# Turning column order into row order in three parts of 64 channels instead of two

## The chip, the cores and the metric

The kernel is one program on one core of a Trainium2 chip. Its time is the device time of one execution, in microseconds. The core has five engines that run their own instruction streams in order: TensorE (PE in the profile), VectorE (DVE), ScalarE (ACT), GpSimd (POOL) and SyncE (SP), which issues all DMAs of this kernel.

## What is computed

Four layers over 4 images of 96 channels and 64 x 64 pixels. Only layer 0 matters here. It is a state-space scan: a depthwise convolution gives `u` with 192 channels, which is read in four orders (rows, columns, and both backwards). In each order a recurrence with 16 states per channel runs over the 4096 positions, and the four results, put back into row order, are added with `Ds` times the input:

```python
def step(hst, inp):
    ut, dt_, bt, ct = inp
    dA = jnp.exp(dt_[..., None] * A[None])
    hst = hst * dA + (dt_ * ut)[..., None] * bt[:, :, None, :]
    y = jnp.einsum('bkdn,bkn->bkd', hst, ct)
    return (hst, y)
...
ys = ys + Ds.reshape(K, DI)[None, :, :, None] * xs
y0 = ys[:, 0].reshape(b, DI, h, w)
y1 = ys[:, 1].reshape(b, DI, w, h).transpose(0, 1, 3, 2)
y2 = jnp.flip(ys[:, 2], -1).reshape(b, DI, h, w)
y3 = jnp.flip(ys[:, 3], -1).reshape(b, DI, w, h).transpose(0, 1, 3, 2)
y = y0 + y1 + y2 + y3
```

A layer norm over the channels and a matrix product follow. Layer 1 is an inverted-bottleneck convolution, layer 2 a Fourier-domain mixer and a feed-forward block, layer 3 linear attention and a feed-forward block.

## The kernel before

**The scan** is the backbone (`scans`, L1216 on). For each image, each order k (0 rows, 1 columns, 2 and 3 backwards) and each of 8 chunks of 512 positions there is a step of 12 slots; 1536 slots in all. A slot handles 64 channels by 8 states in two tiles of 128 x 512. GpSimd forms `db` (L1274), ScalarE the decays `da` (L1284) and copies of the last state (L1308), VectorE runs the recurrence (L1293) and in seven slots of twelve the product with C (L1298). In the other five GpSimd forms that product (L1314). PE sums over the states into the bank `ps_y` (L1338). SP loads the replicated inputs `rep_BC`, `rep_d` and `rep_g` (L1243, L1249) half a step to a step ahead. The result of a step goes to the DRAM tensor `d_y[k]`, 256 rows: rows 0 to 127 are channels 0 to 127, while channels 128 to 191 are there twice, as partial sums over half of the states each, in rows 128 to 191 and 192 to 255.

**Everything else is side work.** Each stage ("front", "turn", "conv", "spectral", "layer_2", "layer_3", "layer_3_turn") is a few Python generators that yield an engine and a planned cost ahead of the instructions they emit. After the scan's own instructions of a slot, `advance` (L1459) takes steps of the first unfinished stage as long as the slot's allowance lasts (L57, `SHARE`: 3.0 us of PE a slot, at most 3.2 saved up; 2.4 of ScalarE; 1.5 of VectorE). A step is taken if half of its cost is left (`fits`, L1446). `yield wait(n)` lets n slots pass. A stage starts only when the one before it is finished. `WORK` (L54) holds the planned cost of each stage, for the rate at which side work is taken. The order of instructions on every engine is that in which they are emitted. Stores are put on a list (`later`) and issued at the next slot's start on the same SP queue as the loads. `in_turn` (L456) emits the matmuls of an item and, one item later, its evacuation; `ahead(1, ...)` (L448) issues an item's loads one item early.

The plan is: front of images 0, 1, 2, then for image 0 turn, conv, spectral, layer 2 and layer 3; front of image 3; the same for image 1, with the turn of image 2 as one stream beside its layer 3; the same for image 2, with the turn of image 3; and last conv and the rest of image 3. What is not done when the scan ends is done after it with all engines free.

**The turn** (`turn`, L631) takes the results of the two column orders, k = 1 and 3, and adds them in row order, together with the forward row order (k = 0) and `Ds` times the input (`d_skip`). It needs three orders of its image to be scanned; for image 3, whose column orders are scanned first, only two, and the rows that wait for order 0 come second. It runs in two parts: channels 0 to 127, and rows 128 to 255. A part has two big tiles, `ya` and `yb` of 128 x 6144 f32. The first 4096 columns of each receive one column order (L641, two DMAs of 2 MB). After `wait(10)` the eight chunks follow: loads of 512 columns of `d_y[0]` (L649) and of `d_skip` (L650) into the spare columns of the tiles, two matmuls whose moving operand steps through the tile column by column (L662; 256 bytes between elements), one with the row order (L664) and one with the skip (L665), whose stationary operand is a diagonal of `Ds`. The stationary operand of the others is an identity, or in the second part two identities of 64 stacked (`two`), which add rows 128 to 191 and 192 to 255. ScalarE copies the sum out (L669), and it is stored to `d_yt`. `scan_outputs` (L679) reads that with the backward row order and begins the "conv" stage.

Of the kernel before, what the change touches and what calls it, by code (L numbers as in the profile page):

```python
# [19 lines left out]
F32 = mybir.dt.float32  # L20
# [3 lines left out]
ALU = mybir.AluOpType  # L24
AX = mybir.AxisListType
PSUM = bass.MemoryType.PSUM

B, C, H, W = 4, 96, 64, 64
L = H * W
# [21 lines left out]

WORK = {"weights": 47.0, "turn": 70.0, "front": 417.0, "conv": 447.0,  # L54
        "spectral": 111.2, "layer_2": 231.0, "product": 1.2, "layer_3": 153.6, "layer_3_turn": 223.6}
RATE = 6.0
SHARE = {"pe": (3.0, 3.2), "act": (2.4, 2.8), "dve": (1.5, 2.0)}  # L57
NQ, NG, NPAIR = 4, HID // 32, H // 2


COLS = [
    ("convb_a", 1), ("convb_b", 1), ("ds_a", 4), ("ds_b", 4), ("one", 1),
    ("lng_a", 1), ("lng_b", 1), ("lnb_a", 1), ("lnb_b", 1),
# [32 lines left out]
def hybrid_kernel(ctx: ExitStack, tc: tile.TileContext, a: dict):  # L96
# [45 lines left out]
    def const(name, rows=slice(0, 128)):  # L142
        return cst[rows, CS[name]]
# [40 lines left out]
    def big(name):  # L184
        if last_room and turns(thirds) == "last":
            return last_room[0].tile([128, 6144], F32, name=name, tag="big", bufs=1)
        return bp.tile([128, 6144], F32, name=name, tag="big", bufs=2)
# [6 lines left out]
    def tmp(name, shape=(128, CH), dtype=F32):  # L194

        if last_room and dtype == F32:
            tag = turns(spare)
            if tag in LAST:
                return last_room[0].tile([128, CH], F32, name=name, tag=tag, bufs=LAST[tag])[:, : shape[1]]
        return bp.tile(list(shape), dtype, name=name, tag="tmp", bufs=TMP)  # L200
# [33 lines left out]
    def split(t):  # L234
        return t.rearrange("p (a b) -> p a b", a=RPC)
# [11 lines left out]
    dtw = small.tile([128, K, DI], F32, name="dtw")  # L247
    taps = small.tile([128, 9, DI], F32, name="taps")
    aneg = small.tile([128, 96], F32, name="aneg")
    ds_a = small.tile([128, 1], F32, name="ds_a")  # L250
    ds_b = small.tile([128, 1], F32, name="ds_b")
    skips = small.tile([128, 2, 128], F32, name="skips")
    w1 = small.tile([128, HID], F32, name="w1")
    w2 = small.tile([128, NT1 + 1, C], F32, name="w2")
    wkv = small.tile([128, 2 * C], F32, name="wkv")
# [29 lines left out]
    def first_weights():  # L285

        take = scratch(big("weights"))

        win = take(128, DI)
        load(win, a["win_t"])  # L290
        load_row(taps.rearrange("p t d -> p (t d)"), "convw")
        load(sel, a["sel"])
        load(dtw, a["dtw"])
        load(cst[:, : CS["grp"].start], a["cst"][:, : CS["grp"].start])
        load(cst[:, CS["grp"].stop :], a["cst"][:, CS["grp"].stop :])
        nc.vector.tensor_copy(ident16, const("ident", slice(0, C))[:, :C])
        nc.vector.tensor_mul(taps, taps, win.unsqueeze(1).to_broadcast([128, 9, DI]))

        pre = take(128, NPRE)
        load(pre, a["pre"])  # L300
        act(aneg, pre[:, PRE["alog"]], AF.Exp)
        nc.vector.tensor_scalar(aneg, aneg, -1.0, None, ALU.mult)
        nc.vector.reduce_sum(ds_a, cols[:, COL["ds_a"]], axis=AX.X)


        nc.vector.memset(ds_b, 1.0)
        nc.vector.reduce_sum(ds_b[:64], cols[:64, COL["ds_b"]], axis=AX.X)
        nc.vector.tensor_scalar(skips[:, 0], const("ident"), ds_a, None, ALU.mult)
        nc.vector.tensor_scalar(skips[:, 1], const("two"), ds_b, None, ALU.mult)

    def later_weights():

# [124 lines left out]
    def later(out, t, then=None):  # L437

        to_store.append((out, t, then))
# [16 lines left out]
    def in_turn(items, make, matmuls, take, evict, depth=2, ready=None):  # L456


        made = []

        def oldest():
            p, item, at = made.pop(0)
            yield take[:3] + (at,)
            evict(p, item)
            free()

        items, n = iter(items), 0
        while True:
            while ready is not None and not ready(n):
                yield wait(1)  # L470
            item = next(items, None)
            if item is None:
                break
            yield make[:3] + (n > 0,)
            p = bank()
            matmuls(p, item)
            made.append((p, item, clock[0]))
            n += 1
            if len(made) == depth:
                yield from oldest()  # L480
        while made:
            yield from oldest()
# [148 lines left out]
    def turn(b):  # L631


        im = b % 2
        early = b == B - 1
        while scanned[b] < (2 if early else 3) * NCH:
            yield wait(1)
        parts = [big("ya"), big("yb")]
        for lo in (128, 0) if early else (0, 128):
            for t, k in zip(parts, (1, 3)):  # L640
                load(t[:, :L].rearrange("p (c l) -> p c l", c=NCH),  # L641
                     d_y[k][im][:, lo : lo + 128, :].rearrange("c p l -> p c l"))

            rows = not (early and lo == 128)

            def fetch(c):
                y, u = (t[:, L + c % 4 * CH : L + c % 4 * CH + CH] for t in parts)
                if rows:
                    load(y, d_y[0][im][c, lo : lo + 128])  # L649
                load(u[: min(128, DI - lo)], d_skip[b][c, lo : min(lo + 128, DI)])  # L650
                return y, u

            whole = lo == 0
            m, add = (128, const("ident")) if whole else (64, const("two")[:, :64])
            skip = skips[:, 0] if whole else skips[:64, 1, :64]

            def added(p, of):
                c, (y, u) = of
                p = p[:m]
                for n, t in enumerate(parts):  # L660
                    rhs = t[:, :L].rearrange("p (w h) -> p h w", h=H)[:, c * RPC : (c + 1) * RPC, :]
                    mm(split(p), lhsT=add, rhs=rhs, start=n == 0, stop=False)  # L662
                if rows:
                    mm(p, lhsT=add, rhs=y, start=False, stop=False)  # L664
                mm(p, lhsT=skip, rhs=u[: skip.shape[0]], start=False, stop=True)  # L665

            def stored(p, of):
                s = tmp("yrow")[:m]
                nc.scalar.copy(s, p[:m])  # L669
                later(d_yt[im][of[0]][lo : lo + m], s)  # L670

            chunks = ahead(1, fetch, range(NCH))

            ready = (lambda n: scanned[b] >= 2 * NCH + min(n + 2, NCH)) if early and rows else (lambda n: True)
            yield wait(10)
            yield from in_turn(chunks, pe(3.8, 1), added, ac(0.6), stored, ready=ready)
            yield wait(2)

    def scan_outputs(b, done):  # L679
# [865 lines left out]
def _layout(v):  # L1545
# [12 lines left out]
    def rows128(x, first=0):  # L1558

        return np.pad(x, [(first, 128 - first - x.shape[0])] + [(0, 0)] * (x.ndim - 1))  # L1560
# [13 lines left out]
    for o in (0, 1):  # L1574
# [1 line left out]
    w2 = tiles(l1["w2"].T, NT1)  # L1576
    cols = {
        "convb_a": l0["conv_b"][:128], "convb_b": np.tile(l0["conv_b"][128:], 2), "one": one,
        "ds_a": ds[:128], "ds_b": ds[128:],
        "lng_a": l0["ln_g"][:128], "lng_b": l0["ln_g"][128:],  # L1580
        "lnb_a": l0["ln_b"][:128], "lnb_b": l0["ln_b"][128:],
        "alog": l0["A_logs"].reshape(K, NI // 2, 32, 2, NJ, 4).transpose(2, 5, 0, 1, 3, 4).reshape(128, 96),
# [68 lines left out]
```

## Time and profile before

| | |
|---|---|
| Median of 3 runs | 6392.89 us (6386.3 to 6405.43) |
| The profiled execution | 6409.81 us |
| Its span, first to last instruction | 6408.0 us |
| Busy: VectorE, GpSimd, PE, ScalarE | 5488.4, 5171.1, 4763.2, 4178.6 us |
| Moved by DMA | 1112 MB, 174 GB/s on average |

The profile gives the instructions of one execution with start, length, line and tile, and for idle time the instruction or DMA that ended it. An f32 matmul is there as two records. Slots can be counted by the L1274 products: the four turns' first column loads are at 1384, 3069, 4201 and 5416 us, in slots 298, 748, 1062 and 1387, and the last product of the scan starts at 5963 us. The trace has no landing times for DMAs, but it has each packet's length.

### The profile page before, as it was taken

To read this page: it belongs to the slowest core of one execution; us is meant where nothing else is said; L and a number is where in the kernel's file an instruction comes from. 1 tells how busy PE (TensorE), PEld (TensorE's weight loads), DVE (VectorE), ACT (ScalarE), POOL (GpSimd) and SP (SyncE) were. 2 spreads that over 40 slices of the span, in tenths; PEclk is the share of its full clock that TensorE was granted. 3 is DMA by queue.
4 is the path that set the end of the run, shared out by engine and by line. 5 is a ranking of instruction groups with operands and counts; after the bars stand their busy time and mean duration, and the time that the engine had idled before them with its cause. 6 is when DMAs were issued, how large, how long until landed. Compare 5 with 4: busy or idle time off the path is not lost. (4 is left out here: it accounts for less than half of the span.)

```text
span 6408.0 us, 84715 instructions
## 1 busy us (share of the span) xinstructions
PE 4763.2 (74%) x27804; PEld 1766.1 (28%) x27804; DVE 5488.4 (86%) x6059; ACT 4178.6 (65%) x8040; POOL 5171.1 (81%) x2743
## 2 busy tenths in 40 slices
PE   6633767757987776686589877767988786867998
PEld 2100212111223532121122254211223632112274
DVE  5979898988999889999899988988999889799345
ACT  5743777765675677887566667856675677665435
POOL 4757878878999889987999988987999888899200
PEclk9855978868998877797799988878998877878999
DMA  5644565666644544456775455465644545555201
GB/s 186 210 159 148 184 205 194 200 222 230 190 158 157 193 161 144 162 195 213 250 222 170 150 180 174 144 213 186 195 161 153 198 157 174 185 188 181 95 11 42
DMA packets 434365, 1112.01 MB, mean 174 GB/s; under 512 B 72474, under 2 KB 74240, under 8 KB 432772
## 3 DMA queue, kind: packets, MB, share of 16 engines
q1 hardware_dynamic: 433924, 1106.58, 52.5%
q8 instruction: 221, 3.62, 0.2%
q14 instruction: 220, 1.80, 0.1%
HBM read 873.41 MB, written 237.44 MB: 173 GB/s over the span
## 5 line engine op out<-in xcount | busy, mean ns | idle before, releaser
L1274 POOL TENSOR_TENSOR db<-rep_g,rep_BC 128x1024 f32<-128x1024 f32 x1536 | 3608.6, 2365 | 753.4 <-DVE hc L1293 352.1
L1284 ACT ACTIVATE ps_da<-rep_d,aneg 128x512 f32<-128x512 f32 x3072 | 2062.6, 690 | 460.1 <-DVE hc L1293 351.1
L1293 DVE TENSOR_TENSOR_SCAN ps_da<-ps_da,state,db 128x512 f32<-128x512 f32 x1568 | 1922.4, 1271 | 284.8 <-ACT state L1308 166.3
L1314 POOL TENSOR_TENSOR hc<-hc,rep_BC 128x1024 f32<-128x1024 f32 x640 | 1511.0, 2361 | 48.5 <-DVE hc L1293 3.7
L1293 DVE TENSOR_TENSOR_SCAN hc<-ps_da,state,db 128x512 f32<-128x512 f32 x1120 | 1370.8, 1264 | 135.2 <-issue 41.7
L1338 PE MATMUL ps_y<-hc,cst 128*32 128x512 f32 x6144 | 1004.1, 732 | 524.2 <-POOL hc L1314 215.6
L1298 DVE TENSOR_TENSOR hc<-ps_da,rep_BC 128x512 f32<-128x512 f32 x1792 | 1133.7, 673 | 0.2
L1308 ACT COPY state<-ps_da 128x1 f32<-128x1 f32 x1568 | 247.3, 158 | 452.9 <-DVE hc L1298 452.1
L1338 PEld LDWEIGHTS ps_y<-hc,cst 128*32 128x32 f32 x6144 | 147.3, 118 | 1173.2 <-issue 484.6
L818 PE MATMUL ps_mm<-h,wd 128*32 128x512 f32 x3144 | 359.9, 593 | 7.0 <-ACT r L155 7.0
L552 PE MATMUL ps_mm<-xp,taps 128*128 128x512 f32 x576 | 292.2, 651 | 47.6 <-ACT xp L532 14.2
L1293 DVE TENSOR_TENSOR_SCAN ps_da<-ps_da,db 128x512 f32<-128x512 f32 x224 | 261.0, 1210 | 28.4 <-ACT state L1308 14.3
L795 PE MATMUL ps_mm<-wd,w 128*32 128x512 f32 x2016 | 255.4, 622 | 27.6 <-DMA wd<-x 17.0
L603 PE MATMUL ps_mm<-xd,dtw 128*128 128x512 f32 x256 | 167.4, 745 | 71.1 <-ACT z L625 51.8
L1293 DVE TENSOR_TENSOR_SCAN hc<-ps_da,db 128x512 f32<-128x512 f32 x160 | 186.1, 1203 | 22.9 <-issue 16.4
L877 PE MATMUL ps_mm<-r,cst 128*128 128x512 f32 x214 | 148.9, 785 | 55.8 <-ACT acc L900 20.3
L799 ACT ACTIVATE h<-ps_mm 128x512 f32<-128x512 f32 x267 | 155.7, 596 | 51.9 <-PE ps_mm L795 49.3
L705 PE MATMUL ps_mm<-ypart,cst 128*128 128x512 f32 (+1 forms) x272 | 158.0, 704 | 38.1 <-DMA ypart<-yt 37.4
L990 PE MATMUL ps_mm<-wa,xp 128*64 128x96 f32 x1728 | 135.1, 318 | 66.2 <-DVE d L995 56.6
L618 DVE SCALAR_TENSOR_TENSOR ps_mm<-ps_mm,z 128x512 f32<-128x512 f32 x192 | 131.3, 684 | 60.5 <-ACT z L616 57.7
L612 ACT ACTIVATE z<-ps_mm 128x512 f32<-128x512 f32 x192 | 114.2, 595 | 96.6 <-PE ps_mm L603 48.2
L552 PEld LDWEIGHTS ps_mm<-xp,taps 128*128 128x128 f32 x576 | 115.4, 207 | 222.0 <-issue 158.8
(343 smaller groups left out, 6824.3 us busy)
## 6 DMA issues: line engine op xcount, KB each, us to landing
rep_BC<-bc SPq DMA_DIRECT2D x512, 512.0 KB
rep_g<-du SPq DMA_DIRECT2D x384, 512.0 KB
rep_d<-delta SPq DMA_DIRECT2D x384, 512.0 KB
y<-yt SPq DMA_DIRECT2D x512, 128.0 KB
du<-g SPq DMA_DIRECT2D x128, 256.0 KB
delta<-z SPq DMA_DIRECT2D x128, 256.0 KB
tab<-in_etab SPq DMA_DIRECT2D x112, 256.0 KB
ypart<-y SPq DMA_DIRECT2D x72, 256.0 KB
```

What stands on the lines that cost most here:

```text
L552: mm(p, lhsT=taps[:, t, 0:128], rhs=window(t, c + e), start=t == 0, stop=t == 8)
L603: mm(p, lhsT=dtw[:, o + 2 * part, 0:128], rhs=xd, start=True, stop=True)
L705: mm(p, lhsT=const(name, slice(0, s.shape[0])), rhs=s, start=n == 0, stop=n == len(of) - 1)
L795: mm(p[32 * n : 32 * n + 32], lhsT=w1[:, 32 * g : 32 * g + 32], rhs=xin[:, n : n + 15 : 2, 1 : W + 1], start=True, stop=True)
L818: mm(p[32 * n : 32 * n + 32], lhsT=held["wd"][:, groups[i], o, dx, :], rhs=here[i][:, :, dx : dx + W], start=dx == 0, stop=dx == 2)
L1274: nc.gpsimd.tensor_mul(x["db"], x["step"]["g"][x["i"]], both(x["step"]["BC"][x["j"]][:, 0]))
L1284: act(x["da"][e], x["step"]["d"][x["i"]][:, e], AF.Exp, scale=aneg[:, av : av + 1])
L1293: nc.vector.tensor_tensor_scan(x["h"][e][:, order], x["da"][e][:, order], x["db"][:, e, order], start, ALU.mult, ALU.add)
L1298: x["made"] = nc.vector.tensor_mul(x["hc"][:, e], x["h"][e], x["step"]["BC"][x["j"]][:, 1])
L1308: nc.scalar.copy(to[:, e : e + 1], x["h"][e][:, end : end + 1])
L1314: x["made"] = nc.gpsimd.tensor_mul(x["hc"], x["hc"], both(x["step"]["BC"][x["j"]][:, 1]))
L1338: done = mm(y[32 * q : 32 * q + 32], lhsT=const("stack"), rhs=x["hc"][:, e], start=first or (x["pass"] == 0 and x["j"] == 0), stop=last or ...
```

## The change

The turn runs in three parts of 64 channels (`lo` = 0, 64, 128; for image 3 the third comes first). There is one big tile: its rows 0 to 63 receive order 1 and its rows 64 to 127 order 3, in two DMAs of 64 rows and 1 MB. One matmul with `two` as stationary operand then adds both orders. The row order and the skip of a chunk go to rows 0 to 63 and 64 to 127 of one spare stretch of the tile, 64 rows and 128 KB each, and a second matmul takes both, with a stationary operand `skips[:, r]` of an identity above a diagonal of `Ds`. The planned PE cost of a chunk is 2.7 instead of 3.8. The constants `ds_a`, `ds_b` and `skips` become `ds` and a `skips` of three blocks.

The third part reads rows 128 to 191 of `d_y` only. Rows 192 to 255, the second half of the state sums of channels 128 to 191, are left out of what the turn adds for orders 1 and 3, and for images 0 to 2 also for order 0.

```diff
-WORK = {"weights": 47.0, "turn": 70.0, "front": 417.0, "conv": 447.0,
-        "spectral": 111.2, "layer_2": 231.0, "product": 1.2, "layer_3": 153.6, "layer_3_turn": 223.6}
+WORK = {"weights": 47.0, "turn": 79.2, "front": 417.0, "conv": 447.0,
+        "spectral": 111.2, "layer_2": 231.0, "product": 1.2, "layer_3": 153.6, "layer_3_turn": 232.8}
...
-        nc.vector.reduce_sum(ds_a, cols[:, COL["ds_a"]], axis=AX.X)
-
-
-        nc.vector.memset(ds_b, 1.0)
-        nc.vector.reduce_sum(ds_b[:64], cols[:64, COL["ds_b"]], axis=AX.X)
-        nc.vector.tensor_scalar(skips[:, 0], const("ident"), ds_a, None, ALU.mult)
-        nc.vector.tensor_scalar(skips[:, 1], const("two"), ds_b, None, ALU.mult)
+        nc.vector.memset(ds, 1.0)
+        nc.vector.reduce_sum(ds[64:], cols[64:, COL["ds"]].rearrange("p (r k) -> p r k", k=K), axis=AX.X)
+        for r in range(3):
+            nc.vector.tensor_scalar(skips[:, r], const("two")[:, :64], ds[:, r : r + 1], None, ALU.mult)
...
-        parts = [big("ya"), big("yb")]
-        for lo in (128, 0) if early else (0, 128):
-            for t, k in zip(parts, (1, 3)):
-                load(t[:, :L].rearrange("p (c l) -> p c l", c=NCH),
-                     d_y[k][im][:, lo : lo + 128, :].rearrange("c p l -> p c l"))
-
-            rows = not (early and lo == 128)
+        t = big("ya")
+        for r in (2, 0, 1) if early else (0, 1, 2):
+            lo = 64 * r
+            for at, k in ((0, 1), (64, 3)):
+                load(t[at : at + 64, :L].rearrange("p (c l) -> p c l", c=NCH),
+                     d_y[k][im][:, lo : lo + 64, :].rearrange("c p l -> p c l"))
+
+            rows = not (early and r == 2)
+            held = slice(0 if rows else 64, 128)

             def fetch(c):
-                y, u = (t[:, L + c % 4 * CH : L + c % 4 * CH + CH] for t in parts)
+                u = t[:, L + c % 4 * CH : L + c % 4 * CH + CH]
                 if rows:
-                    load(y, d_y[0][im][c, lo : lo + 128])
-                load(u[: min(128, DI - lo)], d_skip[b][c, lo : min(lo + 128, DI)])
-                return y, u
-
-            whole = lo == 0
-            m, add = (128, const("ident")) if whole else (64, const("two")[:, :64])
-            skip = skips[:, 0] if whole else skips[:64, 1, :64]
+                    load(u[:64], d_y[0][im][c, lo : lo + 64])
+                load(u[64:], d_skip[b][c, lo : lo + 64])
+                return u

             def added(p, of):
-                c, (y, u) = of
-                p = p[:m]
-                for n, t in enumerate(parts):
-                    rhs = t[:, :L].rearrange("p (w h) -> p h w", h=H)[:, c * RPC : (c + 1) * RPC, :]
-                    mm(split(p), lhsT=add, rhs=rhs, start=n == 0, stop=False)
-                if rows:
-                    mm(p, lhsT=add, rhs=y, start=False, stop=False)
-                mm(p, lhsT=skip, rhs=u[: skip.shape[0]], start=False, stop=True)
+                c, u = of
+                mm(split(p[:64]), lhsT=const("two")[:, :64],
+                   rhs=t[:, :L].rearrange("p (w h) -> p h w", h=H)[:, c * RPC : (c + 1) * RPC, :], start=True, stop=False)
+                mm(p[:64], lhsT=skips[held, r], rhs=u[held], start=False, stop=True)

             def stored(p, of):
-                s = tmp("yrow")[:m]
-                nc.scalar.copy(s, p[:m])
-                later(d_yt[im][of[0]][lo : lo + m], s)
+                s = tmp("yrow")[:64]
+                nc.scalar.copy(s, p[:64])
+                later(d_yt[im][of[0]][lo : lo + 64], s)
...
-            yield from in_turn(chunks, pe(3.8, 1), added, ac(0.6), stored, ready=ready)
+            yield from in_turn(chunks, pe(2.7, 1), added, ac(0.6), stored, ready=ready)
```

More of the change, by code (lines that the diff above doesn't have):

```diff
@@ L61 @@
 COLS = [
-    ("convb_a", 1), ("convb_b", 1), ("ds_a", 4), ("ds_b", 4), ("one", 1),
+    ("convb_a", 1), ("convb_b", 1), ("ds", 12), ("one", 1),
     ("lng_a", 1), ("lng_b", 1), ("lnb_a", 1), ("lnb_b", 1),
@@ L249, in hybrid_kernel @@
     aneg = small.tile([128, 96], F32, name="aneg")
-    ds_a = small.tile([128, 1], F32, name="ds_a")
-    ds_b = small.tile([128, 1], F32, name="ds_b")
-    skips = small.tile([128, 2, 128], F32, name="skips")
+    ds = small.tile([128, 3], F32, name="ds")
+    skips = small.tile([128, 3, 64], F32, name="skips")
     w1 = small.tile([128, HID], F32, name="w1")
@@ L1578, in _layout @@
         "convb_a": l0["conv_b"][:128], "convb_b": np.tile(l0["conv_b"][128:], 2), "one": one,
-        "ds_a": ds[:128], "ds_b": ds[128:],
+        "ds": rows128(ds.reshape(3, 64, K).transpose(1, 0, 2).reshape(64, 3 * K), 64),
         "lng_a": l0["ln_g"][:128], "lng_b": l0["ln_g"][128:],
```

## The prediction

> **What bounds the kernel now.** I read the busy shares and slices first, then the costliest groups, then a table of stretches around the four turns (found by the line of their first matmul, L662), the waits of GpSimd there, and the PE timeline inside one turn.
>
> ```profile
> L1274 POOL TENSOR_TENSOR db<-rep_g,rep_BC 128x1024 f32<-128x1024 f32 x1536 | 3608.6, 2365 | 753.4 <-DVE hc L1293 352.1
> L1314 POOL TENSOR_TENSOR hc<-hc,rep_BC 128x1024 f32<-128x1024 f32 x640 | 1511.0, 2361 | 48.5 <-DVE hc L1293 3.7
> ```
>
> One slot of the scan holds one L1274 product and on average 640/1536 of an L1314 product: (1536 x 2.365 + 640 x 2.361)/1536 = **3.35 us** of GpSimd. That is the floor of a slot. Is it reached? The stretches (columns: us, then busy us of POOL with its instructions, granted clock, DMA share, GB/s); the first four hold the four turns, the fifth a layer 3 without a turn, the last one convolution work:
>
> ```profile
> 1384.00:1556.00 172.00, 146.93 (x81) 0.77 0.66 229
> 3068.00:3233.00 165.00, 157.90 (x82) 0.79 0.73 252
> 4200.00:4446.00 246.00, 191.31 (x106) 0.84 0.59 200
> 5415.00:5670.00 255.00, 208.40 (x110) 0.77 0.57 194
> 2526.00:2690.00 164.00, 154.00 (x85) 0.75 0.44 147
> 3300.00:3650.00 350.00, 346.96 (x186) 0.95 0.54 172
> ```
>
> Beside the convolution GpSimd is busy 347 of 350 us: there the scan sets the time. In the four turn stretches (838 us together) it idles 25 + 7 + 55 + 47 = 134 us. Layer 3 alone idles 10 us in 164, so about 20 of these belong to the two layer-3 stages, and **a little over 110 us is what turns cost the scan**. Why it idled, in the first and the last of the stretches:
>
> ```profile
> POOL db L1274 <- DMA rep_BC<-bc: 19.3, 3, 9.2
> POOL db L1274 <- DVE hc L1293: 3.4, 2, 2.2
> ...
> POOL db L1274 <- DMA rep_BC<-bc: 30.8, 4, 10.4
> POOL db L1274 <- DVE hc L1293: 9.3, 5, 3.7
> ```
>
> Over all four, DMAs account for 19.3 + 0.8 + 18.1 + 30.8 = 69 us, and VectorE, which itself waits there for ScalarE, for 4.2 + 7.8 + 35.6 + 11.6 = 59 us. ScalarE waits for the turn's matmuls (57.9 us at L669 in the first stretch). These are, per chunk:
>
> ```profile
> 1437.34 1.96 PE L662 MATMUL ps_mm<-ya,cst 128*128 128x512 f32 x2
> 1439.13 1.90 PE L662 MATMUL ps_mm<-yb,cst 128*128 128x512 f32 x2
> 1440.85 1.04 PE L664 MATMUL ps_mm<-ya,cst 128*128 128x512 f32 x2
> 1441.72 1.02 PE L665 MATMUL ps_mm<-yb,skips 128*128 128x512 f32 x2
> 1442.67 1.07 PE L1338 MATMUL ps_y<-hc,cst 128*32 128x512 f32 x8
> ```
>
> From start to start: 1.79 and 1.72 us for the two that read columns at a stride (each f32 matmul is two records), 0.87 and 0.95 for the two in order: 5.33 us a chunk, then 1.00 us of the scan's sums. After the last slot (last L1274 at 5963 us) comes a tail of 445 us, with PE busy 411.
>
> **What the skill says.** (1) "SBUF — State Buffer", section Door 1: partitions 0..63 reach 8 of the 16 DMA ports, 196 GB/s against 328 for 128 partitions at 1 MiB. This trace agrees in kind: of the 2 KB packets while the columns of 128 rows arrive (1482 to 1490 us) nearly all take 80 to 100 ns (median 84); during the 64-row loads and stores of a second part (3178 to 3230 us) 535 of 2240 take 120 to 200. (2) The same page, note on cachelines: a strided read pays per line crossed; here 1.75 against 0.9 us. (3) "TensorE: Matmul & The Clock Gate", section HAM oscillation: PE gaps over about 3.4 us end in the slow clock. Agrees: in the first turn the second in-order matmul took 1.85 us at 1429.4 and 1.02 us six microseconds later. (4) "DMA: Bandwidth & Descriptors", section Queues, rings and completion order: each engine takes descriptors in ring order, so a scan load issued behind a burst waits for it. Agrees: loads of columns issued at 1384 us, then the 9.2 us wait above.
>
> **The change, part by part.** A turn goes from 2 x 8 chunks to 3 x 8.
>
> PE: per chunk one strided and one in-order matmul go, 5.33 -> 1.76 + 0.91 = 2.67 us; a turn 16 x 5.33 = 85 -> 24 x 2.67 = 64 us. The planner prices a chunk at 3.8 now, with 3.0 a slot: two chunks in three slots, so PE needs 5.33/1.5 + 0.5 = 4.05 us a slot, over the floor. At 2.7 it emits one chunk a slot: 2.67 + 0.5 = 3.17 us, under it. Of VectorE's 59 us about 10 are layer 3's own. Of the other 49 I put half on steady chunks and half on first chunks (the longest VectorE gap, 9.5 us, is a first chunk). Steady: 24 -> 5. First chunks: the loads go out with the matmul, so PE waits for them (7.1 us at 1427), behind it the sums L1338, on ScalarE the copy L669 and behind that the decays L1284 and states L1308 for which VectorE waits. One strided matmul fewer covers 1.8 us less of the load, but the chunk is 2.7 us shorter; twelve starts at somewhat less than now: 25 -> 25. **49 -> 30, -19 us**; bounds 0 and 59 (all of it per start, 49 x 12/8): -49 to +10.
>
> DMA: columns 8.4 -> 6.3 MB a turn (the third part leaves rows 192 to 255 unread), chunk loads 7.3 -> 6.3, stores 3.1 as before. But every DMA is now of 64 rows. A burst of 4.2 MB took about 11 us at 84 ns a packet on 16 engines. One of 2.1 MB has 1024 packets, 64 on each engine, at 84 to 160 ns: 5.4 to 10.2 us. So the bursts hardly shorten, and there are 12, not 8. Of the 69 us the eight bursts have 9.2 + 6.0 + 0 + 0 + 3.5 + 5.1 + 9.0 + 8.9 = 42 (5.2 each, 0 to 9 by where in the 12-slot step they fall). Twelve at 4.0: 48, +6. The other 27 us, loads of chunks beside those of the scan: +4, as issues rise from 52 to 78 a turn, 26 x 0.5 us more on SP, past the scan's own loads; a store waiting there for L669 holds these up. **+10 us**; bounds: 12 x 2 and 12 x 9 for the bursts, -18 to +66.
>
> ScalarE: 8 copies more of 0.58 us a turn, 19 us in all; it is busy 74 of 172 us in the first stretch and 163 of 255 in the last, so nothing, and up to 19 if it were full. The weights at the start: one small VectorE operation more, under 1 us.
>
> Slots: a part takes 10 waits + 8 chunks + evict + 2 waits. Counting L1274 products, the turns now start at slots 298, 748, 1062, 1387 and a part has 22 to 24; afterwards about 20, three of them. Turns of images 0 and 1, alone in their stage, grow by about 13 slots each; that of image 2 lies beside layer 3 (64 slots to the next stage), +2. Slots cost nothing by themselves, 1536 stay, but all later side work is 28 slots later. Image 3's turn ends at about 1480, not 1449. Its convolution's first expansion comes 20 slots after the stage starts (slots 346 and 365, 797 and 817, 1126 and 1146), but image 3's now waits for the scan (1460 and 1494). So 1500, not 1494: 6 of 46 slots, in which 35% of four blocks were done; 0.19 block, and the tail does a block in (6125 - 5963)/2.6 = 62 us: **+12 us**; 0 to 40.
>
> The single tile frees one big buffer earlier; the next user starts after the turn anyway: 0.
>
> Sum: -19 + 10 + 12 = **+3 us** on the profiled execution's 6409.8 (span 6408.0), which lies 0.26% above the median of 6392.9. So about 6396.
>
> **The rivals.** *Faster*: PE was the whole matter; VectorE's 49 -> 5, bursts halve to 25, tail +6: -44 - 17 + 6 = -55, about 6338. For it: PE is busy 45 of 45 us from 1430 to 1475. Against: GpSimd still ran 43.6 of 44 us in such a stretch (1512 to 1556). *Slower, half the ports*: bursts of 64 rows stall the scan's rep_BC loads 7.5 us each: 90 - 42 = +48, -19 + 12: +41, about 6434. It decides from 3.75 us a burst on (where 12s - 42 + 4 - 19 + 12 is zero). For it: the packets of 120 to 200 ns; against: two bursts cost nothing now. *Slower, late tail*: the convolution of image 3 comes 20 slots late: 20/46 x 1.4 x 62 = 38, with -19 + 10: +29, about 6422. *Not the same work*: rows 192 to 255 are left out in orders 1 and 3 and, for images 0 to 2, order 0; a gain would owe something to that; its times are those above.
>
> **How the numbers follow.** Forecast 0.36 (6380 to 6412), faster 0.26, half ports 0.22, late tail 0.16. A measurement tells about 0.3% (19 us) from no change. Faster by more: 0.26 + 0.02 of the forecast = 0.28; within: 0.32 of it + 0.04 of the tail = 0.36; slower: 0.22 + 0.12 + 0.02 = 0.36. The range 6345 to 6445 cuts the faster case's lower half and the worst bursts. The forecast's own range is 6380 to 6412.
>
> **What would show it.** L662 matmuls of one tile, 192 records, a chunk of 2.7 us, a chunk a slot; GpSimd's waits for rep_BC no shorter, for VectorE about 20 us shorter; 2 KB packets at 120 to 200 ns in every turn; first L705 of image 3 near slot 1480; a longer tail. Wrong if GpSimd's idle time in the turns falls under 90 us, or if bursts stall over 6 us each.

## The result and the profile after

The changed kernel takes **6344.4 us** (median of 5 runs, 6324.0 to 6358.6) against 6396.7 us (median of 5, 6386.3 to 6405.4, the three of the table ahead among them): ratio 0.991, 95% interval 0.9894 to 0.9927. It is about 52 us faster. The forecast was 6396, no change, with a range from 6345 to 6445; the gain was not foreseen. The profiled execution has a span of 6356.8 us and is, at 6358.6 us, the slowest of its five, 14 us above the median; the one of the kernel before (6409.8 us) lies 13 us above its own.

The groups that make up the floor of a slot did not change (busy time and mean ns of one, then idle time before it):

```profile
L1266 POOL TENSOR_TENSOR db<-rep_g,rep_BC 128x1024 f32<-128x1024 f32 x1536 | 3607.0, 2365 | 689.1 <-DVE hc L1285 323.5
L1306 POOL TENSOR_TENSOR hc<-hc,rep_BC 128x1024 f32<-128x1024 f32 x640 | 1511.2, 2361 | 49.3 <-DVE hc L1285 4.5
```

Only the idle time before the first fell, 753.4 to 689.1 us. The table of stretches for the four turns, from the first column load to the first matmul that reads `d_yt` (us, then busy us of POOL, granted PE clock, DMA share, GB/s):

```profile
1388.00:1605.00 217.00, 200.48 (x111) 0.68 0.71 211
3086.00:3307.00 221.00, 201.15 (x107) 0.69 0.71 206
4264.00:4513.00 249.00, 214.63 (x115) 0.80 0.69 202
5461.00:5718.00 257.00, 218.79 (x116) 0.81 0.66 196
```

GpSimd idles 16.5 + 19.8 + 34.4 + 38.2 = 109 us in them. The same four stages of the kernel before, from the first column load to the same matmul (the prediction's stretches end earlier), with 140 us of idle time:

```profile
1384.00:1569.00 185.00, 159.77 (x88) 0.78 0.67 233
3068.00:3246.00 178.00, 165.90 (x87) 0.79 0.72 250
4200.00:4474.00 274.00, 217.99 (x121) 0.82 0.59 198
5415.00:5708.00 293.00, 245.94 (x131) 0.76 0.57 194
```

The waits of GpSimd in the changed kernel's first and last stretch (us in total, times, longest):

```profile
POOL db L1266 <- DMA rep_BC<-bc: 14.5, 3, 9.1
...
POOL db L1266 <- DMA rep_BC<-bc: 17.7, 4, 11.4
POOL db L1266 <- DVE hc L1285: 10.0, 7, 2.7
```

Summed over whole stages, from the gaps ahead of each GpSimd instruction, time went and came like this (us; slots counted by the `db` products; "elsewhere" is the rest of the scan from the first turn on; the conv stages are those in which `scan_outputs` and the convolution run):

| | before | after | difference |
|---|---|---|---|
| Idle in the turns | 140.2 | 109.0 | -31.2 |
| of it ended by a DMA | 69.2 | 58.0 | -11.2 |
| of it ended by VectorE | 60.6 | 43.8 | -16.8 |
| Idle elsewhere | 291.7 | 253.7 | -38.0 |
| of it in the conv stages | 36.4 | 15.9 | -20.5 |
| Last product of the scan, at | 5962.9 | 5897.0 | -65.9 |
| Tail after the scan | 442.8 | 457.4 | +14.6 |

So the scan ends 66 us earlier, and 15 us of that are given back in the tail. With +4.9 us of idle time ahead of the first turn and 1.4 us less of busy time this makes up the whole difference of the two executions, 51.2 us.

These are single executions, and a part of such a table is less certain than its sum. Ahead of the first turn, where all kernels of this document do nearly the same, GpSimd idles 362 to 372 us over the runs; and e7_actq (below), which changes nothing outside the turns, idles 273.8 us there against the 291.7 of the kernel before. So 10 to 20 us between two executions, outside the turns, may be nothing. The same holds for the shares of idle time given for the experiments; their medians decide.

PE inside the first turn (start, length):

```profile
1445.37 1.07 PE L1330 MATMUL ps_y<-hc,cst 128*32 128x512 f32 x8
1446.36 1.91 PE L655 MATMUL ps_mm<-ya,cst 128*64 128x512 f32 x2
1448.10 1.04 PE L657 MATMUL ps_mm<-ya,skips 128*64 128x512 f32 x2
1448.97 1.87 PE L655 MATMUL ps_mm<-ya,cst 128*64 128x512 f32 x2
1450.67 1.04 PE L657 MATMUL ps_mm<-ya,skips 128*64 128x512 f32 x2
1451.64 1.06 PE L1330 MATMUL ps_y<-hc,cst 128*32 128x512 f32 x8
```

One bundle of sums (`ps_y`, x8) belongs to two slots. Two chunks and the sums take 1451.64 - 1445.37 = 6.27 us, just under the floor of two slots, 2 x 3.35 = 6.70 us.

### The profile page after: what moved, and what is told of

Read it like the earlier page. It is cut to its first block, busy times and chain, and to the rows that moved or that the text cites. A ratio compares the mean times of both kernels' runs of the same rounds, so it can differ in the third digit from the quotient of the medians.

```text
span 6356.8 us, 84759 instructions
## 1 busy us (share of the span) xinstructions
PE 4685.7 (74%) x27692; PEld 1723.3 (27%) x27692; DVE 5490.6 (86%) x6059; ACT 4191.3 (66%) x8072; POOL 5169.6 (81%) x2743
## 5 line engine op out<-in xcount | busy, mean ns | idle before, releaser
L1266 POOL TENSOR_TENSOR db<-rep_g,rep_BC 128x1024 f32<-128x1024 f32 x1536 | 3607.0, 2365 | 689.1 <-DVE hc L1285 323.5
L1285 DVE TENSOR_TENSOR_SCAN hc<-ps_da,state,db 128x512 f32<-128x512 f32 x1120 | 1371.7, 1266 | 71.3 <-issue 20.6
L787 PE MATMUL ps_mm<-wd,w 128*32 128x512 f32 x1984 | 254.9, 630 | 29.3 <-DMA wd<-x 20.0
L869 PE MATMUL ps_mm<-r,cst 128*128 128x512 f32 x222 | 152.3, 778 | 56.5 <-ACT acc L892 14.2
L655 PE MATMUL ps_mm<-ya,cst 128*64 128x512 f32 x192 | 183.1, 1044 | 10.4 <-ACT acc L892 10.4
```

The lines of the kernel that those rows point to most:

```text
L655: mm(split(p[:64]), lhsT=const("two")[:, :64], rhs=t[:, :L].rearrange("p (w h) -> p h w", h=H)[:, c * RPC : (c + 1) * RPC, :], start=True, ...
L787: mm(p[32 * n : 32 * n + 32], lhsT=w1[:, 32 * g : 32 * g + 32], rhs=xin[:, n : n + 15 : 2, 1 : W + 1], start=True, stop=True)
L1266: nc.gpsimd.tensor_mul(x["db"], x["step"]["g"][x["i"]], both(x["step"]["BC"][x["j"]][:, 0]))
L1285: nc.vector.tensor_tensor_scan(x["h"][e][:, order], x["da"][e][:, order], x["db"][:, e, order], start, ALU.mult, ALU.add)
```

## The experiments

Every kernel was timed in one session with the kernel before, 4 to 22 executions each; "against before" is the difference of the medians of that session, and where two runs are compared below, it is by this column. The ratios have their 95% intervals. The changed kernel and e3, e6, e11, e12 and e13 leave out rows 192 to 255; e3 also adds the skip and the row order of each chunk twice. All others compute the whole sum.

| | us | against before | ratio |
|---|---|---|---|
| after | 6344.4 | -52.2 | 0.9910 [0.9894, 0.9927] |
| e1_price | 6314.4 | -82.2 | 0.9879 [0.9864, 0.9894] |
| e2_late | 6406.5 | +9.9 | 1.0015 [1.0008, 1.0023] |
| e3_pe_back | 6393.1 | -3.5 | 0.9992 [0.9982, 1.0002] |
| e4_whole | 6461.5 | +64.9 | 1.0104 [1.0090, 1.0118] |
| e5_half | 6393.3 | -0.5 | 0.9995 [0.9984, 1.0006] |
| e6_onedma | 6275.5 | -118.3 | 0.9816 [0.9793, 0.9839] |
| e7_actq | 6390.0 | -3.8 | 0.9992 [0.9982, 1.0001] |
| e8_wait6 | 6344.4 | -49.4 | 0.9920 [0.9900, 0.9940] |
| e9_best | 6377.1 | -19.5 | 0.9972 [0.9962, 0.9982] |
| e10_whole54 | 6412.2 | +15.7 | 1.0024 [1.0010, 1.0039] |
| e11_two_less | 6501.7 | +114.5 | 1.0178 [1.0164, 1.0192] |
| e12_same_slots | 6321.0 | -74.7 | 0.9885 [0.9871, 0.9900] |
| e13_two_less | 6319.2 | -76.6 | 0.9874 [0.9858, 0.9891] |

### The pace of the chunks: e1, e2, e3, e7, e8

**e1_price** changes one number of the kernel before, the planned PE cost of a chunk:

```diff
-            yield from in_turn(chunks, pe(3.8, 1), added, ac(0.6), stored, ready=ready)
+            yield from in_turn(chunks, pe(5.4, 1), added, ac(0.6), stored, ready=ready)
```

> The kernel before with one number changed: the planned PE cost of a turn's chunk is 5.4 us (what its four matmuls take) and not 3.8. A chunk then comes every second slot, 5.33/2 + 0.5 = 3.17 us of PE a slot as in the changed kernel, but data, DMAs and number of matmuls stay. Theory 'pace' (chunks whose matmuls last longer than a slot hold up ScalarE's copy, SP's stores behind it and the scan's loads behind those): most of the gain is here already, 25 to 45 us faster than before. Theory 'less work' (fewer bytes, rows 192 to 255 left out, fewer matmuls): no gain, 0 to 10 us slower from 8 slots more a turn. Theory 'place' (side work merely falls on other slots of the step): a gain only if 8 slots do what 13 did, not to be foretold.

Measured: -82.2 us, more than the pace theory asked for and more than the whole change brings. What the price does stands in PE's order. In the kernel before, 16 of the 48 bundles of two slots that hold chunks hold two of them; with 5.4 all 64 chunks stand one to a bundle. A doubled bundle of the kernel before:

```profile
1449.00 1.06 PE L1338 MATMUL ps_y<-hc,cst 128*32 128x512 f32 x8
1450.00 1.96 PE L662 MATMUL ps_mm<-ya,cst 128*128 128x512 f32 x2
...
1454.38 1.02 PE L665 MATMUL ps_mm<-yb,skips 128*128 128x512 f32 x2
1455.24 1.88 PE L662 MATMUL ps_mm<-ya,cst 128*128 128x512 f32 x2
...
1459.53 1.02 PE L665 MATMUL ps_mm<-yb,skips 128*128 128x512 f32 x2
1460.48 1.07 PE L1338 MATMUL ps_y<-hc,cst 128*32 128x512 f32 x8
```

It takes 1460.48 - 1449.00 = 11.48 us where GpSimd needs 6.70: 4.8 us over. A bundle with one chunk takes 6.33 us. Paid in full, 16 x 4.8 = 77 us is what the doubled bundles cost; idle time in the turns fell from 140.2 to 71.0 us, by 69. The turns' stretches of e1:

```profile
1382.00:1581.00 199.00, 181.69 (x101) 0.77 0.70 239
3075.00:3273.00 198.00, 188.64 (x100) 0.78 0.71 246
4205.00:4463.00 258.00, 235.26 (x128) 0.85 0.64 215
5408.00:5665.00 257.00, 235.37 (x124) 0.83 0.65 216
```

The new price also makes each turn longer and moves all later side work; e8 below takes that apart.

**e2_late** moves the chunks six slots later (`wait(16)` for `wait(10)`) at the old price, to see whether the place and not the pace makes the gain.

> The kernel before with wait(16) in place of wait(10) ahead of each part's chunks: the turns get 12 slots longer, as in the changed kernel, and everything after them lies as late; nothing else differs. Theory 'place': faster by 30 us or more. Theories 'pace' and 'less work': no gain; the tail grows by about 12 us, so 0 to 20 us slower than before.

Measured: +9.9 us, as the theories 'pace' and 'less work' have it; the tail grew by 22 us. The place by itself is not the gain.

**e3_pe_back** gives the changed kernel back the PE time that it saves, in the same slots: the last matmul of each chunk is issued twice.

```diff
+                mm(p[:64], lhsT=skips[held, r], rhs=u[held], start=False, stop=False)
                 mm(p[:64], lhsT=skips[held, r], rhs=u[held], start=False, stop=True)
```

> The changed kernel with the last matmul of each chunk done twice (the skip and row order are added twice, so the sum is another), at the same planned cost of 2.7: PE has 2.67 + 0.91 + 0.5 = 4.08 us a slot in a turn's chunks, as much as before the change (4.05). Theory 'pace': 25 to 45 us slower than the changed kernel. Theories 'less work' and 'place': under 10 us slower, as loads and slots are the same.

Measured: +48.7 us over the changed kernel, a little above the pace theory's upper end. Its timeline of PE:

```profile
1441.70 1.07 PE L1331 MATMUL ps_y<-hc,cst 128*32 128x512 f32 x8
...
1445.31 1.02 PE L658 MATMUL ps_mm<-ya,skips 128*64 128x512 f32 x2
...
1448.74 1.02 PE L658 MATMUL ps_mm<-ya,skips 128*64 128x512 f32 x2
1449.69 1.06 PE L1331 MATMUL ps_y<-hc,cst 128*32 128x512 f32 x8
```

A bundle now takes 7.99 us, 1.29 over the floor. The changed kernel's order has 45 bundles with two chunks: 45 x 1.29 = 58 us at most, and idle time in the turns rose by 46.7 (109.0 to 155.7). So the same rule holds from both sides: most of what a bundle of two slots takes beyond 6.70 us is paid (69 of 77 us in e1, 47 of 58 here).

**e7_actq** issues the turn's stores from ScalarE's queue instead of SP's, to see whether the late copies harm the scan through stores that block its loads.

> The kernel before, only that ScalarE issues the 16 stores of a turn itself after its copy, so that SP never waits for that copy with the scan's loads behind. Two routes are open for the theory 'pace'. Route through SP (late chunk, late copy, store waiting at the head of SP, late rep_BC): most of the gain of e1, 30 to 60 us faster than before. Route through ScalarE (late chunk, copy waiting on ScalarE, late decays and states, VectorE waits): within 10 us of before, as ScalarE waits for the same matmuls as ever.

Measured: -3.8 us, with an interval that takes in no change. Stores on SP are not the main route: idle time ended by DMAs in the turns did fall, from 69.2 to 56 us, but that ended by VectorE rose from 60.6 to 70. That leaves ScalarE's own order as the likely route (copy, then decays and states, then VectorE), which was argued and not isolated. ScalarE's waits at the turn's copies fit it: 153 us in the kernel before and 75 in e1, 122 in the changed kernel and 211 in e3.

**e8_wait6** is e1 with `wait(6)`, so that the turns start in slots 298, 748, 1062 and 1394, nearly those of the kernel before: the price alone.

> The kernel of e1 with wait(6) in place of wait(10): a turn is 8 slots shorter. If only lateness counts, image 3's convolution starts as early as before the change and the tail is 12 to 16 us shorter, so about 6300. Rival: six slots, 20 us, are too short for 4.2 MB beside the scan's loads; PE then waits for the columns at each start with the sums and ScalarE behind it: 0 to 30 us slower than e1.

Measured: -49.4 us, 33 short of e1, at the edge of the rival's range. The tail is 18 us shorter than e1's, as the first theory said. PE does wait longer for the first chunks' loads, as the rival said (40 us at L664 against 26), but in the turns this leaves only 3 us more of idle time; the loss against e1 is outside them (289.7 us idle against 245.1). The turns' stretches of e8:

```profile
1383.00:1553.00 170.00, 156.97 (x87) 0.79 0.73 254
3048.00:3221.00 173.00, 164.89 (x86) 0.79 0.74 255
4177.00:4428.00 251.00, 221.22 (x121) 0.85 0.62 213
5395.00:5643.00 248.00, 224.42 (x119) 0.85 0.63 215
```

Idle: 13 + 8 + 30 + 24 = 75 us. The price at unchanged places takes 66 us from the turns and, by the stage sums, 2 us from everything else; by medians it is worth 49, as the profiled execution of the kernel before lies 16 us above its median of that session. By what ended it: VectorE 60.6 to 36.6, DMA 69.2 to 29.1. **More than half of what the profile put down to DMAs went with PE's overrun.**

### The ports: e5 and e6

**e5_half** is e1 with each 128-row column load split into two of 64 rows, nothing else.

```diff
-                load(t[:, :L].rearrange("p (c l) -> p c l", c=NCH),
-                     d_y[k][im][:, lo : lo + 128, :].rearrange("c p l -> p c l"))
+                for at in (0, 64):
+                    load(t[at : at + 64, :L].rearrange("p (c l) -> p c l", c=NCH),
+                         d_y[k][im][:, lo + at : lo + at + 64, :].rearrange("c p l -> p c l"))
```

> The kernel of e1 (before, chunks priced at 5.4) with each column load of 128 rows issued as two of 64 rows; bytes, matmuls and slots stay. Theory 'half the ports' (64-row DMAs run at about half the rate, so a burst lasts some 20 us and not 11, and the scan's rep_BC loads behind it are later): 15 to 40 us slower than e1. Theory 'number of chunks and parts only' (what the changed kernel loses against e1 comes from three starts a turn instead of two): within 8 us of e1.

Measured: +81.7 us over e1; both theories were far too low. GpSimd's waits in its first turn:

```profile
POOL db L1275 <- DMA rep_BC<-bc: 37.5, 2, 20.9
```

The same in e1:

```profile
POOL db L1274 <- DMA rep_BC<-bc: 15.5, 2, 9.0
```

Idle time ended by DMAs in the turns went from 36.1 to 116.7 us.

**e6_onedma** does the reverse to the changed kernel: the results of orders 1 and 3 go to one DRAM tensor, so that one DMA of 128 rows fills both halves of the tile. The scan's stores of these orders go to that tensor as well.

```diff
+    d_cols = images("cols_", [NCH, 4, 2, 64, CH])
...
-            for at, k in ((0, 1), (64, 3)):
-                load(t[at : at + 64, :L].rearrange("p (c l) -> p c l", c=NCH),
-                     d_y[k][im][:, lo : lo + 64, :].rearrange("c p l -> p c l"))
+            load(t[:, :L].rearrange("p (c l) -> p c l", c=NCH),
+                 d_cols[im][:, r].rearrange("c k p l -> (k p) c l"))
...
```

> The changed kernel with the results of both column orders in one DRAM tensor, in groups of 64 rows, so that a part's columns arrive in one DMA of 128 rows and 2 MB instead of two of 64 rows; all else as changed. Theory 'half the ports': a burst lasts about 6 us and not 10; GpSimd's waits for DMAs in the turns fall from 58 to about 35 us, 10 to 25 us faster than the changed kernel. Theory 'number of chunks and parts only': within 8 us of it.

Measured: -66.1 us against the changed kernel, by far more than the 10 to 25 expected. The DMA view of the 24 us from the first burst of a turn on, in 40 slices (busy share in tenths, GB/s), of the changed kernel:

```profile
DMA  2889779999999999999999999999999992111119
GB/s 113 222 242 116 154 283 273 222 201 195 195 205 191 232 215 195 205 201 188 208 198 212 222 181 307 410 403 416 423 416 423 416 396 116 58 51 51 48 51 201
```

and of e6:

```profile
DMA  5889999999999999999989973201149821111100
GB/s 212 266 229 195 345 365 403 372 379 413 406 410 410 437 403 416 416 423 423 416 348 287 355 300 130 68 27 38 31 143 396 328 82 48 55 48 55 48 0 0
```

Both have the same 2.1 MB of columns in them. In 64-row loads they move at about 200 GB/s and only then do the scan's loads go through at 410; in one 128-row load everything moves at about 410 from the start, and the engines are free again 5 us earlier. The busy digits are 9 in both: **the busy share hides it, the GB/s row shows it.** The packets show it too, in every burst: from 3 to 11 us after a burst's first issue, the median packet of 2 KB takes 84 to 86 ns in all bursts of the kernel before, e1 and e6, and 166 to 178 ns in all of the changed kernel and e5. It is the rows and not the number of DMAs: a burst is two DMAs both in the kernel before and in the changed one. The Trainium skill, "SBUF — State Buffer", section Door 1, has the same for a single DMA to partitions 0 to 63 and to all 128 (196 against 328 GB/s at 1 MiB); here the ratio is about one half (200 against 410). GpSimd's waits in e6's first turn:

```profile
POOL db L1266 <- DVE hc L1290: 3.8, 1, 3.8
POOL db L1266 <- DMA rep_BC<-bc: 3.1, 1, 3.1
```

3.1 us for DMAs, 14.5 in the changed kernel. Over all turns: idle 109.0 to 53.7 us, of it for DMAs 58.0 to 14.2.

### The rows left out: e4, e9, e10, e11, e12, e13

**e4_whole** gives the changed kernel rows 192 to 255 back: its third part has two tiles of 128 rows, as the second part of the kernel before, at the old price.

```diff
...
-                mm(split(p[:64]), lhsT=const("two")[:, :64],
-                   rhs=t[:, :L].rearrange("p (w h) -> p h w", h=H)[:, c * RPC : (c + 1) * RPC, :], start=True, stop=False)
+                for n, tile_ in enumerate(tiles):
+                    mm(split(p[:64]), lhsT=const("two")[:, :64],
+                       rhs=tile_[:, :L].rearrange("p (w h) -> p h w", h=H)[:, c * RPC : (c + 1) * RPC, :], start=n == 0, stop=False)
...
-            yield from in_turn(chunks, pe(2.7, 1), added, ac(0.6), stored, ready=ready)
+            yield from in_turn(chunks, pe(3.8 if r == 2 else 2.7, 1), added, ac(0.6), stored, ready=ready)
```

> The changed kernel with its third part as the second part was before: two tiles of 128 rows, rows 192 to 255 read and added, four matmuls at a planned cost of 3.8; parts one and two as changed. Theory 'less work', in the form that the rows left out bring the gain: all of it gone, within 10 us of before. Theory 'pace': a third of the chunks is over a slot's PE again and a turn has 4 slots more, 10 to 25 us slower than the changed kernel, so half of the gain or more remains.

Measured: +117 us over the changed kernel, 65 over the one before. Neither theory came near, and the run mixes two things: the rows, and once more a chunk of 5.33 us priced at 3.8. Two runs take them apart. **e10_whole54** is e4 with 5.4 for 3.8, **e9_best** is the same third part on top of e6's 128-row loads (only that its row order comes in two loads of 64 rows a chunk, not in one of 128).

> e4_whole with one number changed: the third part's chunk, two tiles and 5.3 us of PE, is priced at 5.4 and not 3.8. Theory 'price and ports': the chunk no longer runs PE over the floor of a slot, most of e4's excess of 117 us over the changed kernel goes, 6350 to 6395, GpSimd idle in the conv stages under 25 us. Rival 'work': within 20 of e4's 6461, since the same rows are loaded and added, and the side work is later still.

> Three parts of 64 channels with column loads of 128 rows as in e6_onedma, and the third part whole: the rows 192 to 255 that the changed kernel and e6 leave out come in a second tile (one more DMA of 128 rows and 2 MB a turn, one more strided matmul a chunk, for images 0 to 2 one more load of 64 rows and one more in-order matmul), and the third part's chunk is priced at 5.4, what it takes. Theory 'price and ports' (what e4_whole lost was a chunk of 5.3 us priced at 3.8 and more loads of 64 rows; the rows themselves cost little): 6280 to 6315, that is 5 to 40 over e6, GpSimd idle in the turns 55 to 75 us, conv stages under 20. Rival 'work' (e4's +117 over the changed kernel is what the left-out rows cost): 6350 to 6400.

Measured: e10 +67.9 us over the changed kernel, between the two theories: the price was worth 49 of e4's 117, the rows 68. e9 +98.8 us over e6: there the rival 'work' was right in its number. e10 is 0.24% slower than the kernel before. **With all its work, the change is no gain.** But "work" needs care: the scan ends 6.7 us earlier in e10 than in the changed kernel (5890.3 against 5897.0) and all of the loss is in the tail, 457.4 to 531.6 us. In e9 25 us are in the scan and 79 in the tail, against e6, in the profiled executions. PE in the tail, in the table of stretches (us, busy us with instructions, clock, DMA share, GB/s), of the kernel before, the changed one and e10:

```profile
5963.00:6408.00 445.00, 411.44 (x4080) 0.98 0.14 43
```

```profile
5897.00:6356.00 459.00, 425.93 (x4206) 0.98 0.14 42
```

```profile
5890.00:6424.00 534.00, 505.00 (x4672) 0.99 0.15 44
```

PE is busy 92 to 95% of it: side work that didn't fit beside the scan is done here. At 5.4 a chunk of the third part comes every second slot instead of every slot, so the part takes 16 slots for its chunks and not 8, every turn gets longer, and image 3's convolution comes later. Its first expansion (L795; L787 after) against the tail, in all runs but e11:

| first expansion of image 3, slot | tail, us |
|---|---|
| 1494: before, e8, e13, e7 | 442.8, 440.0, 447.4, 448.5 |
| 1501 to 1503: e6, e12, e5, after, e1, e3, e2 | 455.7, 456.6, 457.1, 457.4, 458.3, 459.1, 465.2 |
| 1517: e4 | 501.9 |
| 1532: e10, e9 | 531.6, 535.1 |

From the kernel before to e10 that is 88.8 us in 38 slots, **2.3 us a slot**.

**e11_two_less** was to leave the rows out of e1's two parts alone.

> e1_price, the two-part turn, with the changed kernel's omission alone: its second part takes rows 128 to 191 only and leaves out rows 192 to 255 in orders 1 and 3 and, for images 0 to 2, in order 0. Its one tile receives order 1 in rows 0 to 63 and order 3 in rows 64 to 127, skip and row order share one stretch, two matmuls a chunk, priced at 2.7; the first part stays whole at 5.4. Theory 'the rows' (the changed kernel is ahead of the kernel before because it leaves these rows out, which saves 21 us of PE a turn and some 6 slots a turn; three parts by themselves bring nothing): 6220 to 6280, so 35 to 95 under e1, with the first expansion of image 3 about 25 slots before e1's 1502 and a shorter tail. Rival 'three parts' (the shape of the turn helps and the rows are worth little in it): within 25 of e1, 6290 to 6340.

Measured: 197 us over e1, a miss of both. Its timeline tells why (PE, the last chunks of image 3's turn):

```profile
5550.43 1.90 PE L673 MATMUL ps_mm<-yb,cst 128*128 128x512 f32 x2
...
5877.61 1.97 PE L673 MATMUL ps_mm<-ya,cst 128*128 128x512 f32 x2
```

The loads of the last chunk went out, but the planner placed its matmul only when the scan was over, 94 slots later, and image 3's convolution with it. Why the planner held it back was not found; the run says nothing of the rows. **e12_same_slots** avoids it by pricing both parts at 5.4, which leaves the chunks in e1's slots; **e13_two_less** prices the second part at 2.7 for images 0 to 2, which gives the slots back.

> e11_two_less with its second part priced at 5.4 like the first, so that the turns' chunks are emitted in the slots of e1_price, while rows 192 to 255 are left out as in e11 (and as in the changed kernel). In e11 the last chunk of image 3's turn was held back by the planner until after the scan, which hid what e11 was made for; here it is emitted about slot 1464 as in e1. Theory 'the rows cost slots' (what leaving the rows out is worth, 68 from e10 to the changed kernel and 102 from e9 to e6, comes through earlier slots and a shorter tail, not through the engines' work): at e1's slots nothing is gained, and one part's loads of 64 rows cost 15 to 30, so 6315 to 6345. Rival 'the rows cost work' (PE, DMA): 6250 to 6300, GpSimd idle in the turns well under e1's 71 us.

> e12_same_slots with the second part of images 0, 1 and 2 priced at 2.7, so that image 3's turn starts some 20 slots earlier and its convolution begins near slot 1456 to 1460 as in the kernel before; rows 192 to 255 are left out as in e12. Theory 'the rows cost slots': a tail of 440 to 448 us instead of about 458, and the scan as in e12, so 10 to 25 under e12. Rival 'the rows cost work': within 8 of e12.

Measured: e12 +7.5 us over e1, in the range of the slots theory and 21 us above the rival's: at equal slots, leaving the rows out gains nothing on balance. What the engines' work saves may be hidden there, as one part's columns now come in 64-row loads, for which 15 to 30 us had been expected; the two were not separated. e13: 1.9 us under e12, which fits the rival's number and is no difference. In the profiled executions the tail did get shorter (456.6 to 447.4) as the slots theory says, but the scan ended 14.6 us later (5863.9 to 5878.4), with 16.5 us more of idle time in the conv stages. So where leaving the rows out paid, in the changed kernel against e10, the gain is in the tail, through earlier slots; and slots pay only where the tail's gain isn't lost again in the stages. That the rows cost little as work is likely (e9 idles 12 us more than e6 in the turns) but not shown by itself.

## Why the prediction was wrong

Four steps lead from before to after, by medians and in this order: right price 82.2 down (e1), then three parts in place of two 62.7 up (e1 to e9; in the profiled executions nearly all of it is the tail, 458.3 to 535.1), then columns in 64-row loads 35.2 up (e9 to e10, where two parts of three have them), then rows 192 to 255 left out 67.9 down (e10 to after). Sum -52.2. The forecast had none of these in its true size, and their sum only looks small.

**VectorE 49 -> 30, -19 us.** Right in size: idle time ended by VectorE fell by 16.8. That is the sum alone, and in part luck: the half for first chunks, 25 -> 25, rested on somewhat shorter waits a start, and PE's waits for chunks' loads grew from 27 us with eight starts to 55 with twelve. And this step was made to hold all that PE's pace does, which is more. "PE needs 5.33/1.5 + 0.5 = 4.05 us a slot" is an average; the order has doubled bundles of 11.48 us, and their overrun of some 77 us doesn't show under one engine's name. With the price alone (e8) VectorE's share fell by 24 us and the DMAs' by 40.

**DMA +10 us.** This is the step that failed: measured -11.2. "Over all four, DMAs account for 69 us" was taken as the transfers' own cost, and "the other 27 us" as loads that would only grow, to 31; 12 us of them are left in the changed kernel. They were PE's pace under another name: with the pace mended in the old layout, 29.1 to 36.1 us are left in all (e8, e1), nearly all of it behind the eight bursts. The twelve bursts themselves came out as forecast: the waits behind them sum to 46 us, 3.8 each, against 48 and 4.0, though their packets took some 170 ns, more than the 84 to 160 it reckoned with. But the forecast asked only what they cost beside the old bursts, +6, not what the ports cost: with 128-row loads all DMA waits of the turns together are 14.2 us, and the kernel is 66 us faster (e6). Two large terms of opposite sign, pace (49 us down at unchanged places, e8) and ports (66 us up, e6), were put at 19 down and 10 up.

**Outside the turns: 0.** "Slots cost nothing by themselves", and for the scan outside the turns the sum has no term. This is the second step that failed, and the largest miss in the profiles: -38.0 us of idle time, of which 10 to 20 may be the two executions. The price alone at old places gives -2.0 (e8) and later places alone -15.4 (e2), both within that uncertainty; together they give -46.6 (e1). In medians the later places, with the right price, are worth 33 us, net of a longer tail (e8 to e1). In the conv stages the idle time is 28.9 to 43.6 us in the runs with the old places or with the price of 3.8 for a chunk of 5.33 us (before, e2, e4, e7, e8, e13), and 15.5 to 20.6 in the others (e11 apart). Why it takes both was not settled.

**ScalarE and the weights: 0.** No run speaks against it; the 96 copies take 578 ns each, against 582.

**Slots and tail.** Right. The turns start in slots 298, 761, 1087 and 1415 (forecast 298, 761, about 1088, about 1415), image 3's convolution in 1481 (1480), its first expansion in 1502 (1500), and the tail grew by 14.6 us (12). Two us a slot in the forecast, 1.8 measured here and 2.3 from the kernel before to e10.

**The signs.** The prediction named two signs of being wrong, and neither came: idle time in the turns is 109 us and not under 90, a burst costs 3.8 us and not over 6. What failed was a sign of its being right: GpSimd's waits for `rep_BC` in the turns were to be no shorter, and they fell from 63 to 58 us.

**The rivals.** The faster one (6338) came true in its number. Its head, that PE's pace was the matter, was nearer the truth than the forecast (e1, e3, e8), but its terms were not: it had VectorE's waits at 5 us beside layer 3's 10 (43.8 in all) and the bursts halved to 25 (46). So the number is in part luck. *Half the ports* was right about the place and wrong about the price of a burst (7.5 us; 3.8); its loss is real, but stood against a larger gain. *Late tail* put 38 us on the tail, and 14.6 came. *Not the same work* had been named without a time, and it decides the sign: without the omission, and with the third part priced as it costs, the change ends at +15.7 (e10).

**A better kernel.** Of those that compute the whole sum, e1 is the fastest: the kernel before with 5.4 for 3.8, 6314.4 us, 30 us under the changed kernel. e6 is faster (6275.5) but leaves the rows out.

## What to carry to other kernels

Where side work is placed by planned costs, look at the costliest bundle between two steps of the backbone and not at the average: correct a wrong price before the shape of the work is judged, or a new shape gets the credit for it. Idle time "ended by a DMA" need not belong to the DMA: see what is left of it when the engines keep pace. And when a change makes loads narrower, compare with the same load at full width, not with the old one.

## What the runs showed of the hardware that was not expected

A 2.1 MB load to 128 rows beside the scan costs it little: nine of e6's twelve are followed by no wait of GpSimd's for a DMA, the others by 1.3, 3.1 and 5.0 us. The same bytes in two loads of 64 rows cost up to 11.4 us a time, 46 us in twelve (the changed kernel), with DMA engines that look equally busy. Splitting e1's eight bursts of columns, with the same bytes, into loads of 64 rows cost 82 us, 10 us a burst.
